# Adding gated values to residual rows by accumulating DMAs, a pair of chunks at a time

## The chip, the core and the metric

The kernel runs on one core of a Trainium2 chip, in float32 throughout. The metric is the device time of one execution in microseconds (us), as the median of several runs. In the profile PE is TensorE, DVE is VectorE, ACT is ScalarE, POOL is GpSimd and SP is SyncE, which here issues nearly all DMAs.

## What is computed

The input x is (4, 128, 128, 128): four images of 128 channels and 128 x 128 positions. Two layers follow one another, each on a group-normalised copy of its input, with a residual sum:

```python
# layer 0
x = x + L0(gn(x))
# layer 1
x = x + L1(gn(x))

def L0(v):                  # _block on v, plus _block on v with rows and columns exchanged
    t = tokens(v)                           # (positions, channels)
    t = ln(t, ln0)
    y1 = ln(t, ln1)
    t = t + (sigmoid(y1) * y1) @ W_out.T
    y2 = ln(t, ln2)
    wht = y2 @ W_whiten.T
    k = square(relu(wht @ W_key.T))         # 128 -> 512 hidden
    kv = k @ W_value.T                      # 512 -> 128
    r = sigmoid(wht @ W_recep.T)
    return image(t + r * kv)

def L1(v):                  # 3x3 convolution, scaled by a gate from the channel means
    return (conv3x3(v, weight[0]) + bias[0]) * se(mean(v))
```

Every position of the block is treated alone, so the block on the exchanged image gives the exchange of the same result, and layer 0 adds twice one block.

## The kernel before

**Tiles.** An image is cut into blocks of 16 rows, and a block into four chunks of 512 positions; two chunks make a pair (`g`, 64 pairs in all, 16 for each image). The residual rows of a block lie in a tile `x` with channels on the partitions. Before the change chunk `r` of a block is every fourth row from row `r` on (`chunk_rows`). The same rows are also loaded with positions on the partitions, in a tile `xd` (`load_turned`, L728, four DMAs for each block), for the three layer norms.

**The steps of a pair** (`layer0`): the group norm's scale and shift on `xd` (L757), a 32x32 transpose on VectorE (`ut`), statistics (L770), roots on GpSimd (`rs`, L820), scale and shift on ScalarE (`t` and `z`, L839), gain and shift on GpSimd (L908, L911), a turn to channels (on TensorE, `zt` L942, for pairs below 22, by a round trip through memory from there on), SiLU (L934, L947), attention matmuls (`att`, L954), the sum on VectorE (L959), a third norm, whose factors go through memory to a tile `R`, and a turn of `t` to channels by a round trip (`td`, `ts`, `tt`). Then for each chunk: `tt` times `R` is the input `y` of the next matmuls (L1015), `tt` is added to the residual rows by GpSimd (L1026), four key matmuls `pk` (L1033) with a relu on ScalarE (L1038) and a square on ScalarE (L1044) or VectorE (L1050), the receptance matmul `pr` (L1058) with a tanh on ScalarE into the gate tile `r` (L1063), four value matmuls `kv` (L1071), the product of gate and value on VectorE (L1080), the sum of that product into the residual rows on GpSimd (L1086), and statistics of the rows for the second layer's group norm (L1094). When a block's four chunks are done, its rows are stored (`xo`, L1101).

**The second layer** (`conv`) loads such rows back (`xc`) and computes the 3x3 convolution with a Winograd form along the rows: six combinations of rows on VectorE (L1179 to L1193), six times three matmuls (L1203 to L1205), and sums on VectorE (L1222 to L1239). It runs one image behind the first layer, interleaved with it; the last image's convolution has nothing beside it.

**The start.** The first image is loaded once for its statistics alone (`xf`, L446), VectorE aggregates them (L493), two groups of small matmuls (`pm`, `pv`, L498) spread them, and the first block can go on from there. Matmuls without use (`busy`, L411) fill TensorE's gaps at the start; `FIRST_FILL` puts some of them (`hot`) behind the landing of blocks 6 and 7 of the statistics' input.

**The order of the work.** The order on every engine is written ahead of time by a planner (`Plan.order`). Every operation is entered by `op` with an engine, a cost, a priority (`SHIFT` by its name, added to the pair's number), what it reads and writes, and the buffers it makes; the planner takes the operation that can start first, and by priority among those within a short look-ahead (`LOOK`, `HASTE`). `ROOM` tells how many buffers each tag has: `r` two chunk-sized gate tiles, `h` six tiles of hidden values, `zd` and `td` two each. `SQUARES` tells for each of a pair's two chunks and four hidden parts which engine squares it (A ScalarE, D VectorE), for pairs below `SQUARES_AT` = 17 and for the others. The engines then run their queues in order, with waits where the data demand it.

Of the kernel before, what the change touches and what calls it, by code (L numbers as in the profile page):

```python
# [23 lines left out]
    "R": -94.694, "Rc": 15.085, "Rm": -2.646, "S": 24.009, "T": -84.8, "Tz": -36.19, "W": -22.14,  # L24
    "ab": 37.315, "att": 1.644, "b": 31.731, "bn0": 11.794, "bn1": -17.35, "bn2": -15.592,
    "bx": 49.609, "c": 7.82, "cag": 6.719, "cav": -18.068, "cd": -103.804, "cp": -37.768,
    "cp1": -27.368, "cpm": -17.233, "cpr": -71.755, "cpv": -65.194, "cre": 48.407, "crt": -73.005,
    "csg": -26.086, "csp": -39.311, "cth": -29.247, "cve": 53.942, "e": 12.136, "e0": 14.7,
    "e1": -70.81, "e2": -55.971, "edge": 60.492, "fw": 14.887, "g": -16.106, "gag": -13.379,
    "gnb": -14.148, "gpm": -2.701, "gpv": -23.531, "grt": -1.635, "gsp": -6.989, "gve": -30.013,  # L30
    "hot": -13.329, "in": 26.361, "in0": 105.375, "kv": 3.816, "late": 12.753, "m0": 23.5,
    "m1": -101.213, "o": -54.585, "pk": 3.497, "pq": -18.954, "pr": 3.288, "q": -106.007,
    "raw": -61.508, "rc": -6.337, "re": -93.796, "silu": -97.676, "sq": -115.033, "sqd": -34.912,
    "t": -2.49, "tD": -49.255, "tR": 16.588, "tW": -20.948, "th": -60.823, "tt": 105.266,
    "u": 16.271, "us": -19.465, "ut": 67.807, "ut2": 9.337, "uw": -50.513, "v": 57.985, "w": 117.982,
    "w0": 44.736, "w1": -43.048, "w2": -6.943, "x": 70.181, "x1": -70.076, "xc": 6.78, "xd": 2.407,
    "xf": -58.371, "xo": -10.863, "xs": -54.606, "y": 24.867, "z": 15.121, "zD": 21.243,
    "zR": 18.813, "zW": -13.966,
}
SQUARES = (("DDAA", "DDAA"), ("AAAA", "AAAA"))  # L40
TAIL_BANKS = ("Bkv", "Btr", "Btr", "Bh", "Bconv", "Bh")
TAIL_HOMES = ("xc", "xc", "x", "x", "x", "xc", "xc", "x")
CONV_AT, CONV_STEP = 2.0, 2.0
LOOK = {'PE': 0.018, 'DVE': 0.087, 'ACT': 0.048, 'POOL': 0.004, 'SP': 0.048}
HASTE = 31.975
SQUARES_AT = 17
ROOM = dict(
    x=3, xd=2, xs=2, ut=3, t=7, z=2, y=2, zd=2, zc=2, td=2, tt=2, R=2, y2=2, h=6, r=2, xc=2, vt=3, v=4,
# [3 lines left out]
BACKLOG = 1.96  # L52
FIRST_U_ON_DVE = (2, 3)


XF_BUS, FIRST_XD, LATE_AT = 3.4, -25, -5
FILL_UNTIL, FILL_STEP = 330, 1.2
FIRST_FILL = {6: 3, 7: 2}
# [29 lines left out]

class Plan:
# [4 lines left out]
    ISSUE, LAUNCH, LANES = 0.38, 0.9, 8  # L94
# [29 lines left out]
    def order(self):  # L124
# [41 lines left out]
        while done < n:  # L166
# [38 lines left out]
            if e == "SP":  # L205
                free[e] = st + self.ISSUE
                bus = max(bus, st + self.LAUNCH) + o["bus"]
                en = bus + o["dur"]
                lanes.append(max(en, lanes[-1] if lanes else 0.0))
            else:  # L210
                free[e] = st + o["gap"]
                en = st + o["dur"]
                if o["port"]:
                    if e == "DVE":
                        dve_port = (st, en)
                    else:
                        pool_port = (st, en)
# [25 lines left out]
def conv_preact_kernel(  # L243
# [42 lines left out]
        z=[P, SUB, C], y=[P, CH], y2=[P, CH], h=[P, CH], r=[P, CH],  # L286
        xc=[P, BLK_ROWS + 2, W], vt=[P, Q, W], v=[P, Q, W], yt=[P, Q, W], uw=[P, 3, P],
        st=[P, N, 3], rs=[P, N], nb=[P, N], four=[P, 4, N], rrow=[P, 4 * N],
        **{i: [P, SUB, PAIR, P] for i in ("zd", "zc", "td", "tt", "R")},
# [15 lines left out]
    def staged(name, n, src=None):  # L305
        t = sb.tile([P, n], F32, tag="h", name=name, bufs=ROOM["h"])
        if src is not None:
            nc.scalar.dma_start(t, src)
        return t
# [112 lines left out]
    READ, WRITE = (0, 0.85), (0, 0.4)  # L422

    def op(name, eng, cost, prio, emit, reads=(), writes=(), new=(), port=False, bus=0.0):
        return plan.op(name, eng, cost, prio + SHIFT.get(name, 0.0), emit, reads, writes, new, port, bus)
# [5 lines left out]
    def chunk_rows(t, r):  # L431
        return t[:, r : BLK_ROWS : PER, :]
# [105 lines left out]
    def conv_setup(b, at):  # L538
# [90 lines left out]
        for i in (1, 2, 3, 4, 0, 5):  # L629
# [10 lines left out]
            )  # L640
            if i in TAP:
                op("ut2", V, (0.21, 0.29), at, lambda i=i: tapped(i), [(t, 0)], [(t, 0)], (), True)

# [67 lines left out]

    def over(row):
# [8 lines left out]
    def load_turned(k):  # L721
        t = ("xd", k)
        src = rows_of(k).rearrange("(q j) (a r) w -> a j q (r w)", q=SUB, a=SUB)

        def load(a):
            if a == 0:
                make(t, "xd")
            nc.sync.dma_start(T[t][32 * a : 32 * a + 32], src[a])  # L728

        for a in range(SUB):  # L730
            op(
                "xd", D, READ, (2 * k if k else FIRST_XD) + 0.01 * a, lambda a=a: load(a), [(t, "n")] if a else (),
                [(t, a), *([(t, "n")] if a == 0 else ())], [(t, "xd")] if a == 0 else (), bus=1.45,
            )

    def layer0(g):
# [3 lines left out]
        if p * PAIR % PER == 0:  # L740
# [6 lines left out]
            for q in range(SUB):  # L747

                on_dve = k == 0 and q in FIRST_U_ON_DVE

                def lay(q=q, on_dve=on_dve):
                    rs, nb = gn0[b]
                    scale, bias = rs[:, q : q + 1], nb[:, q : q + 1]
                    if on_dve:
                        nc.vector.tensor_scalar(T[xd][:, q], T[xd][:, q], scale, bias, ALU.mult, ALU.add)
                    else:
                        nc.scalar.activation(T[xd][:, q], T[xd][:, q], AF.Identity, bias=bias, scale=scale)  # L757

                op(
                    "u", V if on_dve else A, (0.61, 0.7) if on_dve else (0.705, 0.82), g, lay, [(("gn0", b), 0), *((xd, a) for a in range(SUB))],  # L760
                    [(xd, ("u", q))],
                )
# [117 lines left out]
        for h in range(PAIR):  # L880
            r = (p * PAIR + h) % PER

            def turn(h=h, r=r):
# [5 lines left out]
                "ut", V, (0.61, 0.7), g, turn, [(xd, ("u", q)) for q in range(SUB)],  # L889
# [105 lines left out]
        for h in range(PAIR):  # L995
# [28 lines left out]
            def add_t(channels=channels, r=r, eng=nc.gpsimd if on == G else nc.vector):  # L1024
                xs = chunk_rows(T[xt], r)
                eng.tensor_tensor(xs, channels(), xs, ALU.add)  # L1026

            op("S", on, SLOW if on == G else FAST, g, add_t, [(tt, 0), (xt, r)], [(xt, r)], (), port)
            for j in range(NH):
                pk, hh = ("pk", g, h, j), ("h", g, h, j)  # L1030
# [6 lines left out]
                def relu(pk=pk, hh=hh, j=j):  # L1037
                    nc.scalar.activation(make(hh, "h"), T[pk], AF.Relu, bias=kbias[:, j : j + 1])  # L1038

                op("re", A, (0.572, 0.69), g, relu, [(pk, 0)], [(hh, 0)], [(hh, "h")])  # L1040
                if square_on(g, h, j) == "A":

                    def square(hh=hh):
                        nc.scalar.activation(T[hh], T[hh], AF.Square)  # L1044

                    op("sq", A, (0.52, 0.63), g, square, [(hh, 0)], [(hh, 0)])
                else:

                    def square(pk=pk, hh=hh, j=j):
                        nc.vector.scalar_tensor_tensor(  # L1050
                            T[hh], T[pk], kbias[:, j : j + 1], T[hh], ALU.add, ALU.mult
                        )

                    op("sqd", V, (0.605, 0.685), g, square, [(hh, 0), (pk, 0)], [(hh, 0)])
            pr, gate, kv = ("pr", g, h), ("r", g, h), ("kv", g, h)
# [265 lines left out]
```

## Time and profile before

| | us |
|---|---|
| median of 3 runs | 1743.63 (1743.13 to 1743.8) |
| the profiled execution | 1742.63 |
| its span, first to last instruction | 1740.9 |
| TensorE busy | 1690.7 (97%) |
| VectorE busy | 1424.9 (82%) |
| ScalarE busy | 1293.8 (74%) |
| GpSimd busy | 1184.0 (68%) |
| the 128 sums into the residual rows on GpSimd (L1086) | 169.8 |

A group's row on the page gives the line, the engine, the operation, the tiles written and read, the count, the busy time and the mean duration of one in ns, and then the time that the engine stood idle before such instructions, and what ended it. A matmul in float32 appears as two instructions. Matmuls overlap, so their busy time is more than the distance from one to the next; the chain of waits shows that distance. A row of the table of stretches gives, for each stretch, its length and each engine's busy time with its count of instructions, then the clock granted to TensorE, the busy share of the DMA engines and what they moved.

### The profile page before, as it was taken

How to read it: one execution, taken by the hardware profiler on the slowest of the kernel's cores; microseconds unless marked ns; L12 is line 12 of the kernel's file. 1: busy time of each engine (PE TensorE's matmuls, PEld its weight loads, DVE VectorE, ACT ScalarE, POOL GpSimd, SP SyncE). 2: the span in 40 equal slices, each digit the busy share in tenths (PEclk: the TensorE clock that was granted, in tenths of full speed). 3: DMA queues.
4: the chain of work that ended last, by engine and by line, in shares of the span. 5: the costliest groups of instructions: out<-in, count | busy, mean ns of one | idle time of the engine just before them, and what ended most of it. 6: DMA issues, size and time to landing. Idle time of an engine off the chain costs nothing.

```text
span 1740.9 us, 18709 instructions
## 1 busy us (share of the span) xinstructions
PE 1690.7 (97%) x4872; PEld 815.7 (47%) x4872; DVE 1424.9 (82%) x2619; ACT 1293.8 (74%) x2656; POOL 1184.0 (68%) x1085
## 2 busy tenths in 40 slices
PE   5899999999999999999999999999999999999999
PEld 2444544444444445444445445454544444444443
DVE  5898888788889967798998887888897766448986
ACT  1999998898988887889889877998887875440000
POOL 1778887788987885879777886988878773310000
PEclk9999999999999999999999999999999999999999
DMA  9366675466577777578778877577776565215321
GB/s 326 91 213 202 193 219 194 145 206 230 153 250 246 252 230 236 199 232 247 250 245 245 254 238 240 178 218 236 241 254 199 183 204 176 101 75 224 154 98 73
DMA packets 140170, 354.66 MB, mean 204 GB/s; under 512 B 19079, under 2 KB 78750, under 8 KB 122782
## 3 DMA queue, kind: packets, MB, share of 16 engines
q1 hardware_dynamic: 139472, 352.99, 63.1%
q8 instruction: 39, 0.64, 0.2%
q14 instruction: 69, 0.57, 0.1%
q10 hardware_dynamic: 590, 0.46, 0.1%
HBM read 230.31 MB, written 123.07 MB: 203 GB/s over the span
## 4 chain that ended last, share of the span: by engine, by line
PE 71%; ACT 10%; POOL 8%; DVE 7%; DMA 2%; issue 2%; SPq 0%; ACTq 0%; DVEq 0%; POOLq 0%
PE kv L1071 19%; PE pk L1033 18%; PE m L1203 7%; PE m L1204 7%; PE m L1205 7%; PE att L954 5%; PE pr L1058 5%; ACT t L839 2%; ACT h L1038 2%; POOL rs L820 2%; ACT z L839 2%; DVE st L770 1%; ACT h L1044 1%; POOL x L1026 1%; POOL t L908 1%
## 5 line engine op out<-in xcount | busy, mean ns | idle before, releaser
L1071 PE MATMUL kv<-h,wv 128*128 128x512 f32 x1024 | 525.8, 598 | 4.6 <-DVE r L1080 2.6
L1033 PE MATMUL pk<-y,wk_s 128*128 128x512 f32 x1024 | 480.9, 595 | 4.7 <-ACT h L1038 3.1
L1038 ACT ACTIVATE h<-pk,kbias 128x512 f32<-128x512 f32 x512 | 336.1, 682 | 90.9 <-PE pk L1033 88.3
L1033 PEld LDWEIGHTS pk<-y,wk_s 128*128 128x128 f32 x1024 | 190.0, 190 | 239.3 <-issue 178.1
L1071 PEld LDWEIGHTS kv<-h,wv 128*128 128x128 f32 x1024 | 183.0, 190 | 205.3 <-issue 164.1
L1044 ACT ACTIVATE h<-h 128x512 f32<-128x512 f32 x444 | 267.5, 629 | 2.6
L1086 POOL TENSOR_TENSOR x<-x,r 128x512 f32<-128x512 f32 x128 | 169.8, 1327 | 132.0 <-DVE r L1080 128.5
L820 POOL TENSOR_TENSOR rs<-rs,nhalf 128x8 f32<-128x8 f32 (+1 forms) x134 | 227.2, 1700 | 47.3 <-ACT rs L817 45.1
L839 ACT ACTIVATE z<-t,nb,rs 128x128 f32<-128x128 f32 x512 | 208.7, 489 | 21.8 <-POOL nb L825 20.9
L839 ACT ACTIVATE t<-ut,nb,rs 128x128 f32<-128x128 f32 x512 | 209.7, 488 | 8.5 <-POOL nb L825 4.8
L908 POOL TENSOR_TENSOR t<-t,g 128x512 f32<-128x512 f32 x124 | 161.2, 1301 | 68.0 <-ACT t L839 67.6
L770 DVE BATCH_NORM_STATS2 st<-t 128x6 f32<-128x256 f32 x512 | 187.1, 410 | 22.9 <-POOL t L911 22.7
L1203 PE MATMUL m<-v,uw 128*128 128x512 f32 x384 | 197.7, 596 | 3.9 <-DVE v L1182 3.9
L1204 PE MATMUL m<-v,uw 128*128 128x508 f32 x384 | 195.4, 590 | 0.0
L1205 PE MATMUL m<-v,uw 128*128 128x508 f32 x384 | 194.9, 589 | 0.0
L1015 POOL TENSOR_TENSOR y<-tt,R 128x512 f32<-128x512 f32 x96 | 130.9, 1367 | 59.8 <-PE pk L1033 46.9
L1026 POOL TENSOR_TENSOR x<-tt,x 128x512 f32<-128x512 f32 x124 | 162.5, 1324 | 3.9 <-DMA tt<-ts 3.7
L911 POOL TENSOR_TENSOR t<-t,b 128x512 f32<-128x512 f32 x124 | 162.7, 1319 | 2.6
L954 PEld LDWEIGHTS att<-wo,y 128*128 128x128 f32 x1024 | 130.9, 192 | 51.7 <-issue 33.1
L1063 ACT ACTIVATE r<-pr,rbias 128x512 f32<-128x512 f32 x128 | 87.1, 681 | 72.6 <-PE pr L1058 36.2
L1058 PE MATMUL pr<-y,wr_s 128*128 128x512 f32 x256 | 132.3, 600 | 3.9 <-ACT h L1038 3.0
L954 PE MATMUL att<-wo,y 128*128 128x128 f32 x1024 | 132.8, 276 | 0.4 <-ACT y L947 0.3
(160 smaller groups left out, 2278.6 us busy)
## 6 DMA issues: line engine op xcount, KB each, us to landing
xd<-in_x SPq DMA_DIRECT2D x128, 256.0 KB
x<-in_x SPq DMA_DIRECT2D x32, 1024.0 KB
xo<-x SPq DMA_DIRECT2D x32, 1024.0 KB
R<-rd SPq DMA_DIRECT2D x63, 512.0 KB
ts<-td SPq DMA_DIRECT2D x248, 128.0 KB
tt<-ts SPq DMA_DIRECT2D x62, 512.0 KB
out<-xc SPq DMA_DIRECT2D x31, 1024.0 KB
xc<-xo SPq DMA_DIRECT2D x24, 1152.0 KB
```

Source lines behind the costliest of these rows:

```text
L770: nc.vector.bn_stats(st[:, i : i + 2, :].rearrange("p n f -> p (n f)"), two)
L820: nc.gpsimd.tensor_tensor(T[rs][:, part], T[rs][:, part], nhalf[:, :k], ALU.pow)
L839: nc.scalar.activation(dst[:, s, :], src[:, s, :], AF.Identity, bias=nb[:, i : i + 1], scale=rs[:, i : i + 1])
L954: nc.tensor.matmul(pa[:, ts(m, P)], T[y][:, ts(m, P)], wo2, start=True, stop=True)
L1033: nc.tensor.matmul(make(pk, "Bh"), wk_s[:, ts(j, P)], T[y2], start=True, stop=True)
L1038: nc.scalar.activation(make(hh, "h"), T[pk], AF.Relu, bias=kbias[:, j : j + 1])
L1044: nc.scalar.activation(T[hh], T[hh], AF.Square)
L1058: nc.tensor.matmul(make(pr, "Bh"), wr_s, T[y2], start=True, stop=True)
L1071: nc.tensor.matmul(T[kv], wv[:, j, :], T["h", g, h, j], start=(j == 0), stop=(j == NH - 1))
L1203: nc.tensor.matmul(pc, u[:, 1], vv, start=True, stop=False)
L1204: nc.tensor.matmul(pc[:, :, 1:W], u[:, 0], vv[:, :, 0 : W - 1], start=False, stop=False)
L1205: nc.tensor.matmul(pc[:, :, 0 : W - 1], u[:, 2], vv[:, :, 1:W], start=False, stop=True)
```

## The change

The gated product of a pair is added to the residual rows by one DMA that accumulates into the tile in place of two sums on GpSimd; GpSimd issues it. For that a pair takes eight neighbouring rows of the block, and its chunk `h` every second row of these, so that a pair's destination is one run of 1024 values on each partition. The gate tile `r` holds both chunks of a pair, with two such tiles. The sum of `tt` into the rows (L1026) stays on GpSimd, or on VectorE for the first two pairs.

```diff
+def X_ON(g):
+    return "DMA"
+POUR, POUR_BUS = (1.1, 2.0), 1.2
...
-    def chunk_rows(t, r):
-        return t[:, r : BLK_ROWS : PER, :]
+    def pair_rows(t, p):
+        n = PAIR * CH // W
+        lo = p * n % BLK_ROWS
+        return t[:, lo : lo + n, :]
+
+    def chunk_rows(t, p, h):
+        return pair_rows(t, p)[:, h::PAIR, :]
...
+    def pour(dst, src):
+        dst = dst.rearrange("p r w -> p (r w)")
+        nc.gpsimd.dma_start(dst, src.rearrange("p a h w -> p (a h w)"), accum_op=ALU.add)
...
-            def gated(gate=gate, kv=kv):
-                nc.vector.scalar_tensor_tensor(T[gate], T[gate], 1.0, T[kv], ALU.add, ALU.mult)
...
-                nc.gpsimd.tensor_tensor(xs, xs, T[gate].rearrange("p (a w) -> p a w", a=SUB), ALU.add)
-            op("x1", G, (1.232, 1.272), g, add_gated, [(gate, 0), (xt, r)], [(xt, r)], (), True)
+            def gated(gate=gate, kv=kv, h=h):
+                dst, src = T[gate][:, :, h], T[kv].rearrange("p (a w) -> p a w", a=SUB)
+                nc.vector.scalar_tensor_tensor(dst, dst, 1.0, src, ALU.add, ALU.mult)
...
+            def add_both(gate=gate):
+                pour(pair_rows(T[xt], p), T[gate])
+
+            if X_ON(g) == "DMA":
+                if h:
+                    xs = [(xt, r - 1), (xt, r)]
+                    op("x1", G, POUR, g, add_both, [(gate, 0), (gate, 1), *xs], xs, bus=POUR_BUS)
```

With it come these edits. The turned rows `xd` are loaded by eight DMAs of 128 KB for each block, a set of four for each pair, with runs of 256 values instead of 512:

```diff
-        src = rows_of(k).rearrange("(q j) (a r) w -> a j q (r w)", q=SUB, a=SUB)
+        src = rows_of(k).rearrange("(q j) (p a h) w -> p a j q (h w)", q=SUB, a=SUB, h=PAIR)
+        n = PAIR * P
+        for p in range(PER // PAIR):
+            for a in range(SUB):
...
+                    nc.sync.dma_start(T[t][32 * a : 32 * a + 32, :, n * p : n * p + n], src[p, a])
```

The hidden values lie two parts to a tile, and ScalarE squares two parts in one instruction (`W`):

```diff
-SQUARES = (("DDAA", "DDAA"), ("AAAA", "AAAA"))
+SQUARES = (("DAWW", "DDWW"), ("WWWW", "WWWW"))
...
+                elif how == "W" and not first:
                     def square(hh=hh):
+                        x = T[hh].rearrange("p a b -> p (a b)")
+                        nc.scalar.activation(x, x, AF.Square)
```

Buffers, the fill at the start and the planner's numbers are set anew (all of `SHIFT` too, not shown):

```diff
-LOOK = {'PE': 0.018, 'DVE': 0.087, 'ACT': 0.048, 'POOL': 0.004, 'SP': 0.048}
-HASTE = 31.975
+LOOK = {'PE': 0, 'DVE': 0.106, 'ACT': 0.181, 'POOL': 0, 'SP': 0.25}
+HASTE = 42.849
-    x=3, xd=2, xs=2, ut=3, t=7, z=2, y=2, zd=2, zc=2, td=2, tt=2, R=2, y2=2, h=6, r=2, xc=2, vt=3, v=4,
+    x=3, xd=2, xs=2, ut=3, t=7, z=2, y=2, zd=1, zc=2, td=1, tt=2, R=2, y2=2, h=3, r=2, xc=2, vt=3, v=4,
-BACKLOG = 1.96
+BACKLOG = 5.526
-XF_BUS, FIRST_XD, LATE_AT = 3.4, -25, -5
+XF_BUS, FIRST_XD, LATE_AT = 3.2, -25, -5
-FIRST_FILL = {6: 3, 7: 2}
+FIRST_FILL = {7: 2}
```

The diff also brings branches that are not taken, since the functions that choose them return nothing (`PARITY`, `SUMS_ON_POOL`) or another branch (`S_ON`).

## The prediction

> **What bounds the kernel now.** I read the busy shares on the first lines of the page, then the table of stretches, then the chain of waits, then the order in time of the first 60 us, last the rows of the instructions that the diff edits.
>
> ```profile
> span 1740.9 us, 18709 instructions
> PE 1690.7 (97%) x4872; PEld 815.7 (47%) x4872; DVE 1424.9 (82%) x2619; ACT 1293.8 (74%) x2656; POOL 1184.0 (68%) x1085
> ...
> q1 hardware_dynamic: 139472, 352.99, 63.1%
> ```
>
> TensorE is busy 97%, but a busy matmul here may be one that overlaps or waits, so I price its work by its steps in the chain. Ten `pk` instructions take 4.29 us (0.429 each), sixteen `att` 1.78 us (0.111 each). With these, and 0.43 for a conv instruction, the counts of the page give: `kv` and `pk` 1024 each 440 + 440, `pr` 256 110, `att` 1024 114, the conv's 3 x 384 some 492, the transposes `zt` 20 and a few small ones 4: 1619 us. The first `att` starts at 57.55 us, so 1683 us are there for it. 64 us are slack, and 57 more are the start. Nothing in the diff removes a matmul from the layers, so a gain can only come out of these two sums.
>
> Where does the slack lie? The same prices on the counts of each stretch give 16.8 us lost from 60 to 200, 3.5 from 200 to 300, 11.5 from 300 to 400, 4.1 from 400 to 500, and only 12.3 in the 1100 us from 500 to 1600; the tail loses 8.
>
> ```profile
> core 0: us, PE busy (x) PEld busy (x) DVE busy (x) ACT busy (x) POOL busy (x), PEclk, DMA share, GB/s
> ...
> 100.00:200.00 100.00, 96.59 (x316) 48.41 (x315) 87.21 (x169) 94.65 (x198) 83.41 (x79) 1.00 0.64 195
> ...
> 300.00:400.00 100.00, 94.76 (x309) 47.79 (x308) 82.56 (x162) 89.64 (x186) 80.42 (x76) 0.98 0.56 177
> ...
> 600.00:700.00 100.00, 100.00 (x298) 48.60 (x296) 73.41 (x138) 85.80 (x168) 75.99 (x66) 1.00 0.71 232
> ```
>
> In the first 16 pairs (to 400 us, no convolution beside them) ScalarE is at 90 to 95% and GpSimd over 80%: nearly a second bound. Later the convolution gives TensorE more work for each pair, and the other engines have room.
>
> The start is a chain of its own:
>
> ```profile
> 31.04 1.02 DVE L493 BATCH_NORM_AGGREGATE mv<-st 128x2 f32<-128x192 f32 x1
> 37.74 0.17 DVE L509 COPY mg<-pm 128x5 f32<-128x5 f32 x1 [5.67 <-PE pm L500]
> ...
> 29.49 7.20 PE L411 MATMUL fill<-xf,gmat 128*128 128x512 f32 x10
> 36.53 0.95 PE L498 MATMUL pm<-mv,gturn 128*128 128x1 f32 x8
> ```
>
> The statistics of the first image are aggregated at 32.06 us, but the matmul that needs them, `pm`, stands behind ten warming matmuls in TensorE's queue and starts at 36.53.
>
> **The change, part by part.**
>
> *The adds of the gated values (L1086).* 128 instructions on GpSimd go, and 64 accumulating DMAs of 512 KB come, issued by GpSimd.
>
> ```profile
> L1086 POOL TENSOR_TENSOR x<-x,r 128x512 f32<-128x512 f32 x128 | 169.8, 1327 | 132.0 <-DVE r L1080 128.5 <-DVE mg L509 1.6 <-DMA tt<-ts 1.4
> ...
>   POOL x L1086: 128.5, 42
>   ACT r L1063: 33.2, 23
>   PEld kv L1071: 29.0, 43
>   DVE st L1094: 28.4, 24
> ```
>
> Two adds hold GpSimd for 2 x 1.23 = 2.46 us, by the starts of neighbours in its queue. What GpSimd pays to issue one DMA no row of before shows. From below: SP issues its own in 0.31 to 0.44 us. From above: the 2.46 us that it replaces, or more, as nothing excludes it. The Trainium skill ("DMA: Bandwidth & Descriptors", Latency and other measured facts) puts the first byte of a DMA from GpSimd at some 1 us, for software on its cores writes the descriptors. With 0.4 GpSimd would save 2.1 us a pair, 132 in all; with the page's figure 1.4 a pair, 90 in all. I take 1.1 us, nearer to the page, since the nearest row is of a queue that has hardware for it: 87 us off an engine at 68%. On the path this is worth little. GpSimd is 8% of the chain, but TensorE has only 12 us left to win from 500 to 1600.
>
> The wait that is added: the DMA waits for the products of both halves, and GpSimd's queue stands behind it. It does so now too (128.5 us behind L1080, in an engine with room), and nothing of TensorE's sits straight behind it. The rows then land later: a small transfer in the chain (`rd`) took 2.40 us; 512 KB at 232 GB/s for a share of 0.71, so 327 GB/s, are 1.6 us more; say 4 us after issue instead of 1.3. Who waits: the statistics L1094, the store `xo`, and the next user of the gate tile. The tanh L1063 lost 33.2 us behind L1086, and TensorE's loads 8.3 behind that tanh; now the tile holds a pair and there are two, so tanh of pair g+2 waits for the add of pair g, a whole pair (18 to 25 us) later. I cost the landing at nothing; without that cover it is 3 us for a pair.
>
> A rule speaks against it: the skill ("SBUF — State Buffer", SBUF: two separate sides, the box on "DVE blocks DMA") says that descriptors for GpSimd's DMAs can't be written while VectorE runs a one-source copy or scalar operation in its two-port mode. In this trace the only large instructions of that sort are two at L755, 0.54 us each, at 41 us, before the first add; the loop has two-source operations, transposes and statistics. So the rule's price is about 0 here. If two-source operations did it too, a DMA would be held as an add is: L1086's rows reach from 1.26 to 1.84 us, 0.6 x 64 = 37 us of GpSimd, inside the 87 saved.
>
> *Transfers.* The adds bring 64 x 1.6 = 105 us of the 16 DMA engines, 6% (twice that if reading the destination counts), and `xd` goes in 8 DMAs a block with runs of 1 KB instead of 4 with 2 KB: 128 more issues on SP at 0.38, 49 us. SP mostly stands waiting (289 us for L850's transposes), and the share goes from 63% to about 70%: nothing, unless a round trip falls due with it; the chain has one at 379 us (`ts`, 7.14 us), inside the stretch that loses 11.5.
>
> *Squares.* Widening: a 128-wide ACTIVATE steps 0.385 us and a 512-wide one of the same form 0.705, so 0.83 ns a column; a square of 512 steps 0.52 (two take 1.04 in the chain), of which 0.09 is fixed. A square of 1024 is then 0.95, a saving of 0.09. In the first 17 pairs VectorE's four squares become three: ScalarE has 0.52 + 2 x 0.95 = 2.41 instead of 2.08, +0.33 a pair, 5.6 us in its dense stretch; VectorE has 0.6 less. ScalarE's steps add up to some 17.5 us a pair there (`t` and `z` 3.08 each, eight relus 4.6, squares 2.1, the rest 4.7) and become 17.8, against TensorE's 18.1. From pair 17 on it saves 0.37 a pair.
>
> *One buffer instead of two* for `zd` and `td`: the transpose of the next pair waits for the stores of this one, over ten us earlier; nothing, and some 5 us a time if a store is late. `h` keeps its size.
>
> *The start.* Three of five warming matmuls are dropped, six of the ten instructions at 0.72 us. `pm` would start at 29.5 + 4 x 0.72 = 32.4, just after the aggregate, instead of 36.5: 4.1 us. A less warm TensorE may give back half a us in `pm` and `pv`. The transposed rows for the next step were issued by 31 us, and the step falls at 37, so I expect them there: -3.5 (0 if they are not).
>
> *The order* on all engines is written anew by other priorities; that moves single us both ways in every stretch and is the largest unknown. I put it at 0 with 6 us either way.
>
> The sum: start -3.5; 60 to 200 -1 (GpSimd and VectorE relieved, ScalarE loaded); 200 to 500 0 (GpSimd's relief against ScalarE's 5 us); 500 to 1600 -5, a little under half of the slack there, for GpSimd and ScalarE both have less; tail 0. Together -9.5. The profiled execution took 1742.6 (span 1740.9 and 1.7 around it), 1 us under the median of 1743.6; taken off the median that is 1734.
>
> **The rivals.** *It is a wash*: ScalarE's 5.6 us in the dense stretch takes back the start's 3.5, and TensorE's 99% from 500 on leaves nothing. For: the 90 to 95% of ScalarE to 300 us. Against: its steps still fit under TensorE's. It gives 1743 + 5.6 - 3.5, with a us or two won later, 1743.
>
> *Slower: the issue holds GpSimd longer than the two adds did.* A pair takes TensorE 18.1 us at first (two chunks of nine 512-wide matmuls at 0.86, `att` 0.89, `zt` 0.44), of which GpSimd is busy 0.82, 14.8 us. At 4.5 us a DMA that is 2 more, 17 of 18, in an in-order queue that also holds the normalisation's roots (L820), for which ScalarE waits. I price it as half as much again of the 36 us lost from 60 to 500, +18, less the start's 3.5: 1758. It decides from about 3 us a DMA. For: no row shows the issue; against: the page's 1 us. DMA traffic that delays the round trips would look alike at TensorE.
>
> **How the numbers follow.** About 0.2%, 3.5 us, is what a measurement can tell from none. The forecast: 0.62, with its own range 1724 to 1740. The wash: 0.16, 1740 to 1747. Slower: 0.22, 1747 to 1770. Leaving out about one in ten above and below: 1722 to 1755.
>
> **What would show it.** Right: `pm` at 32 to 33 us; GpSimd's busy time down by the 170 us of L1086; TensorE's waits behind L1063 gone; ScalarE's squares near 0.95 a step; slack from 500 to 1600 about 7. Wrong: `pm` early but `xd` late; gaps over 2.5 us in GpSimd's queue around each DMA; more than 36 us lost from 60 to 500, with ScalarE over 95%; longer waits for `tt` and `zc`.

## The result, and the profile after

The changed kernel takes 1808.71 us (median of 4 runs, 1808.34 to 1809.23), the kernel before in the same comparison 1743.38 (1742.75 to 1743.8): a ratio of 1.0378, interval 1.0364 to 1.0392. It is 65 us slower. The forecast was 1734 us, and the range ended at 1755. It was wrong in sign and in size.

Line numbers are now those of the changed kernel: the accumulating DMA is issued at L750, the statistics of the finished rows are L1185, tanh L1139, the gated product L1160, the store of a block of rows L1192, `kv` L1150, `pk` L1087. The first lines of its page, engines by busy time and queues by their share of the 16 DMA engines:

```profile
span 1807.1 us, 18727 instructions
PE 1712.6 (95%) x4872; PEld 819.7 (45%) x4872; DVE 1418.0 (78%) x2602; ACT 1285.4 (71%) x2451; POOL 1068.7 (59%) x1021
...
q1 hardware_dynamic: 157904, 353.00, 60.0%
q0 software_dynamic: 9216, 33.56, 10.0%
```

No engine became the bound. GpSimd went from 68% to 59%, TensorE from 97% to 95%, and no share rose but that of the DMA engines, from 63% to 70%. So the 65 us are waits, and what waits bring with them. The stretches say where:

```profile
core 0: us, PE busy (x) PEld busy (x) DVE busy (x) ACT busy (x) POOL busy (x), PEclk, DMA share, GB/s
100.00:200.00 100.00, 92.62 (x312) 46.35 (x311) 83.48 (x168) 96.33 (x199) 79.17 (x75) 1.00 0.76 222
300.00:400.00 100.00, 97.12 (x318) 48.15 (x318) 79.64 (x161) 93.53 (x181) 74.00 (x71) 1.00 0.73 211
400.00:500.00 100.00, 92.41 (x267) 44.53 (x266) 79.06 (x142) 82.28 (x162) 73.05 (x71) 0.95 0.72 204
600.00:700.00 100.00, 99.67 (x304) 49.33 (x303) 76.91 (x141) 73.95 (x130) 56.55 (x51) 1.00 0.79 245
800.00:900.00 100.00, 92.56 (x248) 44.05 (x247) 82.08 (x156) 65.90 (x127) 58.47 (x57) 0.95 0.74 225
```

Read the counts in brackets, not the busy shares. In the stretches from 400 and from 800 us the kernel before executes 285 matmul instructions each:

```profile
400.00:500.00 100.00, 98.50 (x285) 46.80 (x285) 85.50 (x165) 87.73 (x185) 87.61 (x78) 1.00 0.64 204
800.00:900.00 100.00, 100.00 (x285) 48.27 (x285) 89.24 (x172) 87.74 (x184) 83.07 (x72) 1.00 0.78 244
```

The changed kernel does 267 and 248 there. A count mixes short and long matmuls, so I price them. With the prediction's price list, TensorE loses 6 us more from 100 to 200, 11 more from 400 to 500, 12 more from 800 to 900, and 3 to 6 more in six of the other stretches to 1500.

What is new among the waits (engine and line, what it waited for, us in total, times, longest), and the same for SP's queue:

```profile
DVE st L1185 <- DMA x<-r: 58.1, 21, 6.5
ACT r L1139 <- DMA x<-r: 15.0, 7, 3.6
...
SPq L1192 <- DMA x<-r: 149.8, 21, 37.5
```

And the DMA itself, its issue on GpSimd (busy us, mean ns) and its way from issue to landing:

```profile
L750 POOL DMA_DIRECT2D x<-r x64 | 58.4, 913 | 85.7 <-DVE r L1160 75.4 <-PE pk L1087 6.4 <-DMA x<-in_x 2.2
DMA to landing us min/median/max: 4.4/5.9/10.8
```

How one such wait reaches TensorE, from the order in time (start, duration, engine, line; in square brackets the idle time before it and what ended it):

```profile
849.05 0.92 POOL L750 DMA_DIRECT2D x<-r  x1 [0.40 <-DVE r L1160]
...
853.60 0.65 DVE L1308 TENSOR_TENSOR p<-xc 128x512 f32<-128x512 f32 x1
858.38 1.29 DVE L1185 BATCH_NORM_STATS2 st<-x 128x6 f32<-128x512 f32 x2 [4.13 <-DMA x<-r]
859.58 1.29 DVE L932 STREAM_TRANSPOSE ut<-xd 128x512 f32<-128x512 f32 x2
860.79 0.65 DVE L1160 SCALAR_TENSOR_TENSOR r<-r,kv 128x512 f32<-128x512 f32 x1
...
861.59 1.22 PE L1150 MATMUL kv<-h,wv 128*128 128x512 f32 x2 [3.19 <-DVE r L1160]
...
862.60 1.91 PE L1358 MATMUL m<-v,uw 128*128 128x512 f32 x2
...
864.31 1.79 PE L1359 MATMUL m<-v,uw 128*128 128x508 f32 x2
```

GpSimd issues at 849.05. The rows are there 9.3 us later. VectorE comes to their statistics 4.13 us too early and stands, though they are only needed when the image is complete. What is urgent is the product L1160, behind them and two transposes in the same queue: it frees the one PSUM bank that `kv` has, and TensorE stands 3.19 us for it.

The wait costs more than itself. The two instructions of L1358 that follow step 1.71 us (862.60 to 864.31), where the same two step 0.86 a little later (871.07 to 871.93). The clock granted to TensorE is half in between, third figure from the right:

```profile
862.44:865.85 3.41, 3.41 (x5) 1.35 (x4) 3.41 (x10) 1.59 (x3) 2.43 (x2) 0.50 0.76 244
```

From the first `att` on, this trace has nine such stretches, 34 us in all, and the kernel before four, 9 us. From the steps of the matmuls in them I estimate 14 us lost at half clock against 3, so some 11 of the 65 us.

Something else goes with the DMA, and it isn't its landing. A VectorE instruction that runs beside GpSimd's work can be held for as long as GpSimd goes on without a break:

```profile
449.18 0.92 POOL L750 DMA_DIRECT2D x<-r  x1 [0.22 <-DVE rrow L840]
...
449.84 1.57 POOL L954 TENSOR_TENSOR t<-t,g 128x512 f32<-128x512 f32 x1
...
452.97 7.57 DVE L1309 TENSOR_TENSOR q<-xc 128x512 f32<-128x512 f32 x1
...
458.64 1.33 POOL L1072 TENSOR_TENSOR x<-tt,x 128x512 f32<-128x512 f32 x1
...
463.50 0.67 DVE L1160 SCALAR_TENSOR_TENSOR r<-r,kv 128x512 f32<-128x512 f32 x1
...
464.23 1.22 PE L1150 MATMUL kv<-h,wv 128*128 128x512 f32 x1 [4.06 <-DVE r L1160]
```

The instruction of L1309 takes 0.68 us in the median and 7.57 here: it ends 0.6 us after the last of GpSimd's row of eight, which began behind a DMA's issue. The gated product stands behind it on VectorE, and TensorE waits 4.06 us. From the first `att` on, ten VectorE instructions take more than 2 us in this trace, 36 us above their medians, and in each case the row on GpSimd holds a DMA's issue. The kernel before has none of them, nor has any run below without the DMA, but for the one in which GpSimd adds whole pairs.

### The profile page after: what moved, and what is told of

The parts are those of the page before. It is cut to its first block, busy times and chain, and to the rows that moved or that the text cites. A ratio compares the mean times of both kernels' runs of the same rounds, so it can differ in the third digit from the quotient of the medians.

```text
span 1807.1 us, 18727 instructions
## 1 busy us (share of the span) xinstructions
PE 1712.6 (95%) x4872; PEld 819.7 (45%) x4872; DVE 1418.0 (78%) x2602; ACT 1285.4 (71%) x2451; POOL 1068.7 (59%) x1021
## 3 DMA queue, kind: packets, MB, share of 16 engines
q1 hardware_dynamic: 157904, 353.00, 60.0%
## 5 line engine op out<-in xcount | busy, mean ns | idle before, releaser
L1150 PE MATMUL kv<-h,wv 128*128 128x512 f32 x1024 | 532.1, 602 | 30.8 <-DVE r L1160 22.0
L1087 PE MATMUL pk<-y,wk_s 128*128 128x512 f32 x1024 | 499.1, 595 | 2.7 <-ACT h L1093 2.5
L1150 PEld LDWEIGHTS kv<-h,wv 128*128 128x128 f32 x1024 | 186.0, 191 | 252.1 <-issue 172.1
L1087 PEld LDWEIGHTS pk<-y,wk_s 128*128 128x128 f32 x1024 | 191.7, 191 | 236.7 <-issue 196.5
L866 POOL TENSOR_TENSOR rs<-rs,nhalf 128x8 f32<-128x8 f32 (+1 forms) x134 | 232.4, 1753 | 104.0 <-ACT rs L863 97.6
L1112 ACT ACTIVATE h<-h 128x1024 f32<-128x1024 f32 x222 | 233.7, 1053 | 1.7
L1358 PE MATMUL m<-v,uw 128*128 128x512 f32 x384 | 201.6, 607 | 7.2 <-DVE v L1299 5.5
L1072 POOL TENSOR_TENSOR x<-tt,x 128x512 f32<-128x512 f32 x124 | 165.1, 1359 | 18.7 <-DMA tt<-ts 18.7
L957 POOL TENSOR_TENSOR t<-t,b 128x512 f32<-128x512 f32 x124 | 167.7, 1365 | 3.4
L1000 PEld LDWEIGHTS att<-wo,y 128*128 128x128 f32 x1024 | 125.8, 192 | 48.8 <-issue 20.4
L837 POOL TENSOR_TENSOR four<-four,nhalf 128x8 f32<-128x8 f32 x63 | 109.1, 1731 | 65.7 <-ACT four L833 65.4
L1160 DVE SCALAR_TENSOR_TENSOR r<-r,kv 128x512 f32<-128x512 f32 x128 | 86.5, 676 | 77.7 <-PE kv L1150 76.7
```

The costliest lines, as they stand in the source:

```text
L866: nc.gpsimd.tensor_tensor(T[rs][:, part], T[rs][:, part], nhalf[:, :k], ALU.pow)
L957: eng.tensor_tensor(T[t], T[t], over(b0), ALU.add)
L1000: nc.tensor.matmul(pa[:, ts(m, P)], T[y][:, ts(m, P)], wo2, start=True, stop=True)
L1087: nc.tensor.matmul(make(pk, "Bh"), wk_s[:, ts(j, P)], T[y2], start=True, stop=True)
L1112: nc.scalar.activation(x, x, AF.Square)
L1150: nc.tensor.matmul(T[kv], wv[:, j, :], T["h", g, h, j // 2][:, j % 2], start=(j == 0), stop=(j == NH - 1))
```

## The experiments

Three theories. *A, waiting*: the rows land late, and in-order queues stand for them. *B, traffic*: the added transfers delay others. *C, the order*: what came with the DMA, above all the newly written order, costs by itself. A fourth, *Q* (GpSimd's own queue), came up on the way. Most runs keep the order of the changed kernel instruction by instruction, so they can be set side by side.

**GpSimd adds the pair at the DMA's place.** The call of the DMA becomes

```diff
-                pour(pair_rows(T[xt], p), T[gate])
+                rows = pair_rows(T[xt], p).rearrange("p r w -> p (r w)")
+                nc.gpsimd.tensor_tensor(rows, rows, T[gate].rearrange("p a h w -> p (a h w)"), ALU.add)
```

> The order on every engine and all other edits stay as in the changed kernel; only at the place of each accumulating DMA GpSimd adds the pair's 1024 values itself, in one instruction of about 2.4 us. Theory A (waiting: the rows land about 6 us after the issue, and VectorE's statistics and SP's stores stand for it in their queues, with the gated products and the round trips behind them): the rows are there after 2.4 us, so the time falls to 1740-1755. Theory B (traffic: the 10% more on the DMA engines delays the other transfers): falls to the same 1740-1755. Theory C (the new order and the other edits, with or without the DMA): stays at 1795-1810.

Measured: 1813.38 us, ratio 1.0403 (1.0388 to 1.0419). No transfer, no landing, and slower still. It does not clear A and B, though, since the add holds GpSimd 2.44 us where the DMA holds it 0.91. The waits for GpSimd show it. First this run, then the run without any adding (below), in the same order:

```profile
DVE st L816 <- POOL t L957: 40.7, 39, 2.8
PEld pr L1132 <- POOL y L1061: 37.1, 37, 2.8
ACT t L885 <- POOL nb L871: 32.7, 21, 3.8
ACT z L885 <- POOL nb L871: 27.1, 19, 4.7
```

```profile
DVE st L816 <- POOL t L957: 17.6, 15, 4.7
PEld pr L1132 <- POOL y L1061: 12.4, 22, 1.8
ACT t L885 <- POOL nb L871: 14.0, 10, 3.1
ACT z L885 <- POOL nb L871: 14.9, 12, 2.6
```

In this order three engines stand for GpSimd, and a longer slot lengthens each of these waits. VectorE is held beside the long adds too: 17 of its instructions take over 2 us here. GpSimd at 59% busy has no room where it counts.

**The DMA adds into the gate tile instead of the rows.**

```diff
-                pour(pair_rows(T[xt], p), T[gate])
+                pour(T[gate].rearrange("p a h w -> p (a h) w"), T[gate])
```

> The same DMA of 512 KB at the same place, but it accumulates into the gate tile itself, so that the gated values are left out of the residual rows and nothing but the tile's next user waits for the landing; order and traffic stay. A: VectorE's 58 us and SP's 150 us of standing for this DMA go, and the time falls to 1745-1765. B: stays at 1795-1810, as the traffic is the same. C: stays at 1795-1810.

Measured: 1794.27 us, 1.0291 (1.0267 to 1.0315). Nothing waits for the rows any more, and only 14 us come back. A alone does not explain the loss.

**The statistics read constants instead of the rows.**

```diff
-                nc.vector.bn_stats(st1[b][:, i, :], chunk_rows(T[xt], p, h))
+                nc.vector.bn_stats(st1[b][:, i, :], wv.rearrange("p j c -> p (j c)"))
```

> Only VectorE's wait is taken away: the statistics read a constant tile of the same size instead of the residual rows, so the second layer's statistics are left out; DMA, stores and order stay. A, if VectorE's queue is the place: falls by 35-60, to 1750-1775, and TensorE's 22 us of waits for the gated product go. A, if SP's queue behind the stores is the place: under 15 us, 1795-1808. B and C: 1800-1810.

Measured: 1788.67 us, 1.0272 (1.0246 to 1.0297). Taking 58 us of waits off VectorE brings 20. That is near to what TensorE got back, for its wait for the gated product was 22.0 us in the changed kernel and is 5.1 here, while tanh's wait for the landing, 15.0 before, stays:

```profile
ACT r L1139 <- DMA x<-r: 18.1, 8, 4.2
...
PE kv L1150 <- DVE r L1160: 5.1, 11, 1.3
```

Part of the 20 may be luck of the moment: the VectorE instruction that took 7.57 us takes 2.64 in this run.

**An eighth of the data.** The DMA adds only the first of a pair's eight rows.

```diff
-                pour(pair_rows(T[xt], p), T[gate])
+                nc.gpsimd.dma_start(
+                    pair_rows(T[xt], p)[:, 0, :], T[gate].rearrange("p a h w -> p (a h) w")[:, 0], accum_op=ALU.add
+                )
```

> Each accumulating DMA moves only the first of its eight rows (64 KB of 512), the other seven sums are left out; order and issue stay. A: landing falls from 5.9 to 3-4 us and only half of the statistics wait for it, 1745-1775. B: the software queue's share falls from 10% to under 2%, and the time to 1745-1760. C: stays at 1795-1810.

Measured: 1780.20 us, 1.0207 (1.0177 to 1.0237). With 64 KB the landing takes 2.3/3.5/8.3 us (least, median, most), and the waits of the statistics for it fall from 58 us to 17. Waits and transfers both shrink here, so the run can't tell A from B; no theory's range for it was met.

**No adding at all, in the order of the changed kernel**: the call is replaced by `pass`.

> Leaves out the adding of the gated values (no DMA, no GpSimd add; the rows lack them); every other instruction of the changed kernel, in the same written order. A (the landing and who stands for it) and B (the transfers) together say that the whole loss comes with the DMA: 1740 to 1755 us. C (the written order and the other edits cost by themselves) says that what the run with an eighth of the data had left stays: 1770 to 1782 us, some 30 us above the kernel before.

Measured: 1758.21 us, 1.0082 (1.0063 to 1.0101). So in this order the DMA is worth 50 of the 65 us. It isn't the DMA as such: GpSimd's own adds in its place were worth 55 (1813.4 - 1758.2). From 800 to 900 us TensorE is back at 297 matmuls:

```profile
800.00:900.00 100.00, 100.00 (x297) 49.44 (x296) 82.22 (x165) 77.31 (x143) 55.09 (x51) 0.99 0.74 231
```

C keeps 14 us, less than I expected of it from the run with an eighth. By the same prices the trace shows 6 us of it from 100 to 200 us, and 6 us in the last image's convolution, behind the last `kv`, where the forecast had put nothing.

**The DMA alone, in the kernel before**: its order, rows and buffers, and one DMA of a chunk for each GpSimd add.

```diff
-                nc.gpsimd.tensor_tensor(xs, xs, T[gate].rearrange("p (a w) -> p a w", a=SUB), ALU.add)
+                nc.gpsimd.dma_start(xs, T[gate].rearrange("p (a w) -> p a w", a=SUB), accum_op=ALU.add)
```

> The kernel before, in its own order and with its own rows and buffers; each of its 128 GpSimd adds of gated values becomes one accumulating DMA of that chunk (256 KB) at the same place. So the DMA alone, without any other edit. A: the statistics and the next tanh of that buffer come some 4 to 5 us after the issue rather than 1.3, in an order that was not written for it: 1780 to 1830 us. C alone (the DMA does no harm, only what came with it): 1740 to 1755 us.

Measured: 2231.89 us, 1.28 (1.2779 to 1.2822), far beyond what A expected. The chunk's rows lie apart, in pieces of 512 bytes. The issue takes 1.32 us, no less than the add it replaces, and the landing 3.8/5.1/12.3 us. Its waits (lines of the kernel before: tanh L1063, statistics L1094):

```profile
ACT r L1063 <- DMA x<-r: 499.7, 114, 11.5
DVE st L1094 <- DMA x<-r: 454.3, 107, 10.8
```

Tanh of the next pair needs the gate buffer some 4 us before it is free, 114 times of 128. The granted clock is 0.925 in this run, so part of the 488 us is TensorE at half pace. This is the price of a landing with no cover. In the changed kernel the gate tile of a pair and the new order hide most of it. I had half seen that, for the gate tile only.

**The hand-set numbers alone**: the kernel before with the changed kernel's `SHIFT`, `LOOK`, `HASTE` and `BACKLOG`.

> The kernel before with the planner's hand-set numbers of the changed one (the due-time shifts, look-ahead, haste, backlog) and nothing else: no DMA, no wide squares, its own buffers. C, if the order those numbers write is what costs: 1765 to 1785 us. If the numbers are harmless and the loss is the DMA's: 1740 to 1758 us. A and B as such say nothing of it.

Measured: 1794.07 us, 1.0289 (1.0267 to 1.0311). The kernel before loses 50 us by them, with no other edit.

**The landing told to the planner, and a third gate tile.**

```diff
-    x=3, xd=2, xs=2, ut=3, t=7, z=2, y=2, zd=1, zc=2, td=1, tt=2, R=2, y2=2, h=3, r=2, xc=2, vt=3, v=4,
+    x=3, xd=2, xs=2, ut=3, t=7, z=2, y=2, zd=1, zc=2, td=1, tt=2, R=2, y2=2, h=3, r=3, xc=2, vt=3, v=4,
...
-    ISSUE, LAUNCH, LANES, LAND = 0.38, 0.9, 8, 0.85
+    ISSUE, LAUNCH, LANES, LAND = 0.38, 0.9, 8, 2.8
```

> The changed kernel with a third gate tile and with a planner that takes a DMA to land 6 us after its issue rather than 4, so the order is written anew. A: what stood for the landing (33 us of the chain) mostly goes, 1770 to 1785 us. C: the order is a different one, of the same kind, 1795 to 1815 us. B alone (the transfers are the same): 1800 to 1810 us.

Measured: 1829.68 us, 1.0493 (1.0474 to 1.0513), a miss for every theory. It did what it was to do, for the statistics' wait fell from 58 us to

```profile
DVE st L1185 <- DMA x<-r: 17.9, 5, 5.4
```

and tanh waits for no landing any more, yet the order that comes of it is 21 us worse. A written order can change by tens of us when two numbers of its model change. Runs whose order was written anew say little on the DMA, and I went back to the fixed one.

**The nearest waiters taken away, step by step, in the fixed order.** First a third gate tile alone, with the planner still writing the order for two:

```diff
-    plan = Plan(ROOM, BEGIN)
+    plan = Plan(dict(ROOM, r=2), BEGIN)
+    ROOM["r"] = 3
```

> The changed kernel in its own written order with a third gate tile (the planner still writes the order for two) and nothing else. A, with the statistics as the first waiter: 1798 to 1808 us, since the tanh waits are 15 us of the profile and the statistics keep theirs of 58. If the gate tile is the main waiter: 1785 to 1795 us.

Measured: 1804.99 us, 1.0358 (1.0336 to 1.0380); hardly any gain, as A had it. Then with constant statistics as well:

> The changed kernel in its own written order, with both nearest waiters on the landing taken away: the statistics of the rows read constant values instead of the rows (so they are not the rows' statistics), and there is a third gate tile, so tanh need not wait for the DMA of the last pair but one. The DMA itself, its issue and its transfers stay. A: nearly all that the DMA costs goes, 1758 to 1770 us (1758 is the run without any adding). B: the transfers still cost, 1780 to 1790 us.

Measured: 1781.95 us, 1.0215 (1.0198 to 1.0232), in B's range. And with the stores reading constants too:

```diff
-                nc.sync.dma_start(spill[b][:, kb * BLK_ROWS : (kb + 1) * BLK_ROWS, :], T[xt][:, :BLK_ROWS, :])
+                nc.sync.dma_start(spill[b][:, kb * BLK_ROWS : (kb + 1) * BLK_ROWS, :], wv[:, 0:1, :].to_broadcast([P, BLK_ROWS, W]))
```

> As the run with constant statistics and a third gate tile, and the stores of the finished rows read constant values too (so what is stored are not the rows), so that SP's queue does not stand for the landing either. What the DMA still has is its issue on GpSimd and its traffic. A: 1757 to 1763 us, the level of the run without adding. B: the level stays 15 us or more above that, 1775 us or higher.

Measured: 1783.18 us, 1.0221 (1.0201 to 1.0242). Taking away SP's 149.8 us behind the landing, the longest row of all, brought nothing that shows. The constant stores move in more pieces, 219,344 packets on that queue in place of 157,904, which may hide a small gain. All waits for the landing together are 1808.7 - 1783.2 = 25 us, with the half-clock stretches behind them. A expected 1757 to 1763, so some 25 us were still open.

**The 25 us that are not waits for the landing.** Three runs on top of the last one. First, only the pair's first row gets its gated values (64 KB, and such a DMA needs the first chunk's product alone):

```diff
-                pour(pair_rows(T[xt], p), T[gate])
+                nc.gpsimd.dma_start(
+                    pair_rows(T[xt], p)[:, 0, :], T[gate].rearrange("p a h w -> p (a h) w")[:, 0], accum_op=ALU.add
+                )
```

Second, constants of full size:

```diff
-                pour(pair_rows(T[xt], p), T[gate])
+                rows = pair_rows(T[xt], p).rearrange("p (s r) w -> p s (r w)", s=2)
+                some = wv.rearrange("p j c -> p (j c)").rearrange("p (o n) -> p o n", o=1)
+                nc.gpsimd.dma_start(rows, some.to_broadcast([P, 2, CH]), accum_op=ALU.add)
```

Third, constants for the first row only:

```diff
-                pour(pair_rows(T[xt], p), T[gate])
+                nc.gpsimd.dma_start(pair_rows(T[xt], p)[:, 0, :], wv[:, 0, :], accum_op=ALU.add)
```

> The run in which nothing waits for the landing (constant statistics, constant stores, third gate tile), and its DMA adds only the first of a pair's eight rows (64 KB of 512). Issue and GpSimd's wait for the gated product stay, the transfers nearly go. B (transfers cost the 25 us): 1758 to 1765 us. Q (GpSimd's queue standing for the gated product, and the issue): 1778 to 1786 us.

> The run in which nothing waits for the landing, and its DMA adds constants of full size (512 KB) to the rows in place of the gated values, so that GpSimd need not wait for the gated product before it issues. Issue and transfers stay. Q, if it is the wait: 1758 to 1768 us. B, or Q if it is the issue alone: 1778 to 1786 us.

> Both: nothing waits for the landing, one row of constants (64 KB) is added in place of the pair's gated values. Only the issue on GpSimd stays. B and Q, if it is the wait: 1758 to 1764 us. Q, if it is the issue of 0.91 us each on GpSimd: 1775 to 1786 us.

Measured: 1774.59 (1.0176, 1.0155 to 1.0198), 1787.61 (1.0254, 1.0233 to 1.0276) and 1772.94 us (1.0171, 1.0152 to 1.0190). GpSimd's 67 us of standing for the gated product cost nothing that shows: with no such wait the full-size run is not faster. It is 4 us slower. Its constants come in more pieces and their issue takes longer, which may hide a small gain:

```profile
L1172 POOL DMA_DIRECT2D x<-wv x64 | 78.3, 1231 | 0.0
q0 software_dynamic: 17408, 33.56, 10.9%
```

What is left with 64 KB of constants is 1772.94 - 1758.21 = 15 us, and whole pairs add about 10 us (1783.18 - 1772.94), or 15 by the two runs with constants. I call the first the issue and the second the transfers, but neither name is shown to be the whole. In favour of the issue, GpSimd has 11% of the chain that ended last in the run with 64 KB of constants, and 4% without any adding. But VectorE's held instructions go with it: seven over 2 us there, 21 us above their medians, and ten, 36 us, with whole pairs, so the 10 us aren't transfers alone. A little of the transfers stays in the "issue" (2.0% of the engines' time against 10.2%), and so do the packets of the constant stores.

**What the adds cost in the kernel before**: they are left out, in its own order.

> The kernel before in its own order, leaving out the adding of the gated values (the rows lack them). It shows what the 128 GpSimd adds, and their place in the chain, cost in the kernel before, and so what any way of taking them off GpSimd could bring in that order. If GpSimd is off the chain there, as the forecast had it after 500 us: 1735 to 1743 us; if the adds hold the statistics and the gate tiles up: 1715 to 1733 us.

Measured: 1745.15 us, 1.0004 (0.9993 to 1.0015). GpSimd falls to 59% here too, as the busy line of this run shows,

```profile
PE 1689.6 (97%) x4872; PEld 815.6 (47%) x4872; DVE 1415.3 (81%) x2619; ACT 1294.2 (74%) x2656; POOL 1022.3 (59%) x957
```

the 33.2 and 28.4 us that tanh and the statistics lost behind the adds are gone, and nothing comes of it. In that order the adds are free, within 3 us. No way of taking them off GpSimd could have made the kernel faster without another order.

**The 14 us of the order and the other edits.** A second `td` buffer in the run without adding, and the changed kernel with GpSimd's adds instead of the DMA, its order written for that (`X_ON` returns "POOL"):

> The changed kernel in its own written order, leaving out the adding of the gated values, and with two td buffers instead of one (the planner still writes the order for one). The run without adding stood 14 us above the kernel before. If the single td buffer holds the turned rows up: 1745 to 1752 us. If it costs nothing, as the forecast had it: 1755 to 1761 us, and the 14 us are the order's and the other edits'.

> The changed kernel with GpSimd adding each chunk's gated values as the kernel before does, no DMA, and the order written anew for that: what the other edits and the hand-set numbers make without the DMA. If only the DMA costs: 1740 to 1755 us. If the numbers write a worse order, as they did for the kernel before (1794 us): 1765 to 1795 us.

Measured: 1756.87 us (1.0076, 1.0054 to 1.0097) and 1802.45 us (1.0346, 1.0311 to 1.0382). The single `td` buffer costs nothing. With a second `zd` as well the tiles no longer fit on the chip, so the single `zd` stays untested. The second figure lies above both theories' ranges: with the changed kernel's numbers an order with adds is as slow as the one with DMAs, as far as the intervals tell. It loses 60 us without any DMA.

Together, each row with what it adds to the row above, from the second row on in the order of the changed kernel:

| | us | adds |
|---|---|---|
| kernel before, without the adds | 1745.2 | |
| changed kernel, without the adding | 1758.2 | 13: the order and the other edits |
| one row of constants, nothing waits | 1772.9 | 15: 64 issues on GpSimd, VectorE held beside them |
| whole pairs, nothing waits | 1783.2 | 10: transfers, and more of VectorE held |
| the changed kernel | 1808.7 | 25: waits for the landing |

By the intervals of the ratios each step is uncertain by 4 to 5 us, and this is one path of several. The planner's numbers alone lost 50 us in the kernel before, and an order written by them for GpSimd's adds lost 60; on that path the DMA in place of the adds is only the last 6. Adding costs 50 to 55 us in the new order, by DMA or by GpSimd, and nothing in the old one. The loss belongs to the adding and the order together.

## Why the prediction was wrong, step by step

- *The landing, "costed at nothing"*: on the path of the table this is the step that failed most, 25 us. It was put at 4 us and measured 5.9 in the median and 10.8 at most. The Trainium skill ("DMA: Bandwidth & Descriptors", Anatomy of one DMA) fits a GpSimd DMA as some 2.0 us plus its bytes at 436 KB per us. An estimate from it is 3.2 us for a pair, and the fastest landing here was 4.4; for 64 KB 2.2 and 2.3. For the fastest ones the page has the small DMA right and the large, accumulating one too short; the medians, beside the kernel's other traffic, are 5.9 and 3.5. The cover was argued for the gate tile only. The prediction names the statistics as a waiter and then forgets that VectorE's queue is in order. Without cover it said 3 us a pair. The profile has 28 such waits (21 and 7), 73.1 us, 2.6 each: the size was right, and the number of them was set to zero.
- *The issue*: 1.1 us was near (0.913, none over 1.07), by luck, for it was drawn from a time to the first byte, which is not the time that GpSimd is held. "On the path this is worth little" was meant of a gain. But in the new order engines stand for GpSimd, and the run with little but 64 issues of 0.91 us is 15 us slower than the one without, while GpSimd's busy time fell by 115 in the change. The prediction asked whether VectorE's instructions hold the DMA up. What the trace shows is the other way round: VectorE held beside GpSimd, 36 us in ten instructions. How much of the 15 us that is stays open. The slower rival was to decide only from about 3 us a DMA.
- *GpSimd's relief, part of -5 from 500 to 1600*: worth 0 by the run without adds. In the old order there was no gain to be had from it, so every cost decided the sign. The trace held a hint: no wait of TensorE's was put down to the adds, and only 8.3 us to the tanh behind them.
- *Transfers at nothing*: some 10 us at most. Their packets took 10.0% of the 16 engines, 2.8 us of all of them for each DMA, near the "twice that" in brackets rather than the 6%; the share of 70% came out. GpSimd's waits for the turned rows `tt` went from 3.7 to 18.7 us, as listed under what would prove it wrong, but they are 19.0 in the run without adding too: that sign belongs to the order, not to the transfers.
- *The order, "0 with 6 us either way"*: with the other edits 13 us when nothing is added, and 50 and 60 us in the two runs that have the new numbers and GpSimd's adds. This term was sized too small by far, and on that path it is the larger failure. The prediction took the order for a matter of its own, but it also decides what the adding costs.
- *The start, -3.5*: in the profiled execution the shift `nb` from the first statistics came at 41.20 us, 0.3 later than before. The order in time of TensorE:

```profile
31.54 3.76 PE L431 MATMUL fill<-xf,gmat 128*128 128x512 f32 x4
35.09 1.71 PE L525 MATMUL pm<-mv,gturn 128*128 128x1 f32 x8
...
38.02 1.84 PE L525 MATMUL pv<-q,gturn 128*128 128x1 f32 x8 [0.80 <-DVE q L538]
```

  The setup's matmuls ended 2 us later and so did the four warming ones begin; each took 0.89 us, not 0.72, and `pm` and `pv` took 1.71 and 1.84 instead of 0.95 and 1.02. The half us given back for a colder TensorE was 1.6. The 0.72 was a mean: six of the ten steps before are 0.85 to 1.0 us and four 0.43 to 0.49, and the four that are left are all of the slow sort. But one execution isn't the rule here. In the 15 traces with this start `nb` comes at 34.9 to 41.8 us, at 37.8 in the median, and in the four with the old one at 39.3 to 41.7. So the 3 us were mostly won, as forecast, and the profiled execution of the changed kernel is one of the late ones.
- *Right*: a wide square steps 0.95 us (1003.29 to 1004.24); the single `td` buffer is free; ScalarE's load in the dense stretch rises (94.65 to 96.33 from 100 to 200). Whether it does harm is open: that stretch loses 6 us more, with and without the DMA.

The slower rival had the direction, not the mechanism: it priced a busy GpSimd from 60 to 500 us. What came was spread over the whole kernel, in four steps of 10 to 25 us each on the path of the table.

What stays open is how the 13 us split between the order, the wide squares and the rows' new layout, and how the 15 and the 10 split between GpSimd's slots, VectorE held and transfers. Waits overlap and can bring half-clock stretches behind them, so another sequence of removals shifts us between the rows.

## What to carry to other kernels

Before you move work off an engine, leave it out altogether, in the same order, and time that: here the bound on the gain was 0, so a gain could only have come from another order. A DMA that takes over a short operation is to be costed by all that stand for its landing, in whichever in-order queue, and by what is queued behind them. Where the order is written for one set of costs, tens of us can come from a change of it: test an edit with the order held fixed, and the new order without the edit. And read one instruction's longest time beside its median; a row's mean hides the few that were held.

## What the runs showed of the hardware

- An accumulating DMA between SBUF tiles: GpSimd is held 0.91 us for 144 packets whether they carry 64 KB or 512 KB, 1.23 us for 272 packets, and 1.32 us for 528. For 144 packets the bytes make no difference; more packets take longer, but not in proportion.
- Its landing is 2.3 us at least for 64 KB and 4.4 for 512 KB, with medians of 3.5 and 5.9 beside the kernel's other traffic: more than half is there whatever the size.
- Its packets took 2.8 us of all 16 engines for 512 KB; at the 327 GB/s of the other traffic, 1.6 us were expected.
- A VectorE instruction on 128 x 512 values, 0.68 us in the median, took up to 7.57 us beside an unbroken row of GpSimd instructions with a DMA's issue in it. In the kernel before none took over 1.9 us from the first `att` on.
- In or just behind waits of 3.19 and 4.06 us TensorE's granted clock fell to half for 3.4 and 6.8 us, and its matmuls took twice their steps (1.71 us for 0.86).
